# A graph attention kernel: weight sums, pair loads and result additions of the second product put elsewhere

## The chip, the cores and the metric

The kernel runs on one core of one Trainium2 chip. The metric is the device time of one execution in microseconds (us), of which the median over runs is given; lower is better. Everything is computed in 32-bit floats.

## The reference

Two graph attention layers on 512 nodes and 768 features, then a residual addition and a layer norm. The first layer has H = 8 heads of 768 features each, the second has one.

```python
def gat_layer(x, W, a_s, a_d, b, edge_index, concat):
    h = (x @ W).reshape(n, H, C)
    alpha_s = einsum('nhc,hc->nh', h, a_s); alpha_d = einsum('nhc,hc->nh', h, a_d)
    e = leaky_relu(alpha_s[src] + alpha_d[dst], 0.2)
    alpha = softmax of e over the edges of one dst
    out = segment_sum(h[src] * alpha, dst)
    return out + b
h = elu(gat_layer(x, W1, a_src1, a_dst1, b1, edge_index, concat=True))     # 512 x 6144
out = gat_layer(h, W2, a_src2, a_dst2, b2, edge_index, concat=True)        # W2 is 6144 x 768
return layernorm(x + out)
```

## The kernel before

The edges are counted once into a dense 512 x 512 matrix, so that attention is dense. Heads go one after another through a pipeline of three kinds of stages on TensorE:

- a *projection*: HS[h] = x @ W1 of a head (512 x 768 times 768 x 768);
- a *mixed* stage: the head's features times its turned attention weights PT, followed by elu, into gT (`mixed`);
- a *second* stage: h2 += gT of this head times its 768 rows of W2 (`second_by_thirds`), while scores of the next head are computed on VectorE and ScalarE and turned by DMA transposes (`turn_out`, `turn_in`).

In the loop `for h in range(H - 1)` come mixed(h), second(h) and, where there still is a head h + 2, its projection. For h = 1 to 5 that is `project_by_thirds`; for h = 0 it is `projection` (fourteen products by halves). The last head (h = 7) is done after the loop by halves (`second`), then come the second layer's attention and the layer norm.

**Products by thirds.** Left operand, weights and result are cut in parts (two row blocks of 256 nodes, three blocks of 256 inputs, three of 256 outputs), and 15 products P0 to P14 of sums of such parts replace 18. Each product is two row tiles times two input tiles: the page counts 8 matmuls for it. The results of products accumulate in five chains, each with one PSUM bank: a (P8), x (P13, P4, P6, P14, P7), b (P9), y (P2, P12, P0, P10, P11, P3), z (P1, P5). After each product the bank's present content is added to, or subtracted from, one part of the destination; the next product of the same chain may not begin before that has read the bank. `STEPS` (L423) names the chain, the part (row block, column block) and the sign of each product.

**How a result gets to its part of h2** (`empty` in `by_thirds`). Either VectorE adds the bank to h2 (L461), or, for the parts listed in `by_dma`, ScalarE copies the bank into a pass buffer (L458) and GpSimd issues an accumulating DMA from there into h2 (L459). Before, the parts are (1, 2), (0, 1) and (0, 2), so the results of P8, P13, P0, P1, P14, P11 and P3 go by DMA: seven in a stage with h > 0, and four in h = 0, where the first result of each part is copied straight into h2 by ScalarE. There are two pass buffers, the halves of `pass_`. In h = 0 `pass_` first holds the left operands P8 and P13; for h > 0 the tile `absent` holds them.

**The weight operands.** Each of the 15 products needs a weight part or a sum of parts. The slot w1 holds those of the second product, the slot w2 those of the projection. A slot has the rows (`w1r`, 6 tiles of 128 x 768: chunk 0 holds P8, P9, P5; chunk 1 P7, P1, P0; chunk 2 P4, P14, P3), and three flat tiles of two squares each: t1 (P13, P12: "the pairs"), t2 (P6, P2) and t4 (P11, P10). Sums are made by loading one part and adding another from memory with an accumulating DMA on GpSimd's queue (L144), by an accumulating DMA between tiles of the slot, or by VectorE (L170):

- from memory: P1 += , P14 += , P13 += , P12 += , P11 += ;
- then P6 = P14 - P4, P2 = P12 - P13, P4 = P13 + P4, P0 = P12 + P0, P10 = part + P1, P3 = P10 - P3, P1 = P6 + P1, P7 = P6 + P7.

In slot w1, before, P6, P2, P4 and P3 are done by VectorE; P0, P10, P1 and P7 by DMA. `load_thirds` issues all loads of a head in this order: six rows (with the adds into P1 and P14 after the 4th and 6th), then the pairs, each with its add, then `rest`: P11, P10 and the add into P0. For the second product both are called after product n = 14 of the second stage of the head before (and once ahead of the loop, at n = 10 there). The sums P6 and P2 are done in the projection at n = 13 and 14, P4 at the end of the mixed stage (`behind`); P10, P1, P7 are issued in `behind_it[2]`, after product n = 2 of the second stage (L1118); P3 at n = 11.

The products of a second stage run in the order P8, P13, P2, P4, P12, P9, P6, P0, P1, P10, P5, P14, P11, P7, P3 (n = 0 to 14). `plan[n]` is what VectorE and ScalarE are given after product n is issued and ahead of its result, `behind_it[n]` what follows its result. Left operand sums (`gsums`) are part of it; so are, for the next head's four query tiles, `score` (ScalarE: L604), `scored` (VectorE: L608, L613; ScalarE: L617) at n = 5, 7, 9, 11 and `out_by_dma` at n = 7, 9, 11, 13 (ScalarE: L862, L865; SP: a transpose, L867). `turn_in` (ScalarE, L870) takes a transpose in.

**Queues.** The order on every engine is that of the program text; an engine waits in order. Plain loads are issued on SP, accumulating DMAs on POOL. SP also carries the transposes, the row of logits (L596, L599) and, for h = 1 to 5, the reload of five left operands of the projection into gT (`reload_x`, L1003), at n = 11, followed at n = 12 by the load of the w2 slot's P11 (`rest_of_thirds`).

Of the kernel before, what the change touches and what calls it, by code (L numbers as in the profile page):

```python
# [37 lines left out]
def gat_pass(  # L38
# [93 lines left out]
    def load_thirds(m, slot):  # L132

        chunks = CHUNKS[slot]

        def part(k, n):
            lo, hi = chunks[k]
            return m[lo * P:(hi + 1) * P, n * TH:(n + 1) * TH].rearrange("(k p) d -> p k d", p=P)[:, ::hi - lo]

        def flat(j):  # L140
            return wpool.tile([P, HK, HALF], F32, name=f"{slot}t{j}").rearrange("p k n -> p (k n)")

        def add_up(o, i):
            nc.gpsimd.dma_start(o, i, accum_op=ALU.add)  # L144

        rows_, pair_ = wpool.tile([P, DC, D], F32, name=f"{slot}r"), flat(1)
        for j, c in enumerate(c for pair in chunks for c in pair):
            nc.sync.dma_start(rows_[:, j, :], m[c * P:(c + 1) * P, :])
            if j == 3:
                add_up(third(rows_, 1, 1), part(1, 2))  # L150
            if j == 5:
                add_up(third(rows_, 2, 1), part(0, 1))
        for j, (k0, k1, n) in enumerate(((0, 2, 2), (0, 1, 0))):
            nc.sync.dma_start(square(pair_, j), part(k0, n))
            add_up(square(pair_, j), part(k1, n))
        raw = {(k, n): third(rows_, k, n) for k in range(3) for n in range(3)}
        B_ = dict(P8=raw[0, 2], P9=raw[0, 0], P5=raw[0, 1], P13=square(pair_, 0), P12=square(pair_, 1),
                  P14=raw[2, 1], P4=raw[2, 0], P0=raw[1, 2], P3=raw[2, 2], P7=raw[1, 0], P1=raw[1, 1])

        def rest():  # L160

            two, four = flat(2), flat(4)
            B_.update(P6=square(two, 0), P2=square(two, 1), P11=square(four, 0), P10=square(four, 1))
            nc.sync.dma_start(B_["P11"], part(0, 1))
            if slot == "w1":
                nc.sync.dma_start(B_["P10"], part(0, 1))
            add_up(B_["P11"], part(1, 1))

            def op(o, a, b, how):
                return lambda: nc.vector.tensor_tensor(B_[o], B_[a], B_[b], op=how)  # L170

            def by_dma(o, i):
                return lambda: add_up(B_[o], B_[i])
            ops = dict(P6=op("P6", "P14", "P4", ALU.subtract), P4=op("P4", "P13", "P4", ALU.add),
                       P2=op("P2", "P12", "P13", ALU.subtract), P3=op("P3", "P10", "P3", ALU.subtract))
            if slot == "w1":
                add_up(B_["P0"], B_["P12"])
                ops.update(P10=by_dma("P10", "P1"), P1=by_dma("P1", "P6"), P7=by_dma("P7", "P6"))
            else:
                ops.update(P10=op("P10", "P5", "P1", ALU.add), P0=op("P0", "P12", "P0", ALU.add),  # L180
                           P1=op("P1", "P6", "P1", ALU.add), P7=op("P7", "P6", "P7", ALU.add))
            return ops
        return B_, rest
# [4 lines left out]
    def load_w2(h, slot="w1"):  # L188
        return load_w(W2, h, slot, w2[h * D:(h + 1) * D, :])
# [10 lines left out]
    first_rows = wpool.tile([P, DC, D], F32, name="w1r")  # L200
    W1[0] = [first_rows[:, :HK], first_rows[:, HK:]]
# [17 lines left out]
    W1[0].append(wpool.tile([P, HK, HALF], F32, name="w1t1"))  # L219
# [3 lines left out]
    def sums_by_dma(W_, m, slot):  # L223

        lo_, hi_, t1_ = W_
        t2, t4 = (wpool.tile([P, HK, HALF], F32, name=f"{slot}t{j}") for j in (2, 4))
# [1156 lines left out]
```

## Time and profile before

| | us |
|---|---|
| median of 3 runs | 723.98 (723.26 to 726.53) |
| the profiled execution, its own time | 719.46 |
| its span, to which the profile's times and shares refer | 717.6 |
| busy: TensorE / its weight loads | 644.5 / 492.7 |
| busy: VectorE / ScalarE / GpSimd | 515.7 / 337.4 / 178.0 |
| DMA: moved, mean rate | 133.46 MB, 186 GB/s |

The profile's page lists groups of instructions: line, engine, operation, output <- inputs, tile shapes, count, then busy time in us, mean ns of one, and the idle time of the engine just before them with what ended it. PE is TensorE, PEld its weight loads, DVE VectorE, ACT ScalarE, POOL GpSimd, SP the engine that issues plain DMAs; a q behind the engine means its sequencer or queue. Digits are dropped from tile names, so w1t stands for w1t1, w1t2 and w1t4, h for h2. In a timeline the bracket tells how long the engine sat idle before an instruction, and what released it.

### The profile page before, as it was taken

The numbers are of one execution on the slowest core, as the hardware profiler recorded it, in microseconds if no ns is written. First come the engines' busy times: TensorE is split into PE (matmuls) and PEld (weight loads), VectorE is DVE, ScalarE is ACT, GpSimd is POOL, SyncE is SP. The second block draws the span as 40 slices with busy tenths as digits, with TensorE's granted clock in tenths as the row PEclk, the third lists the DMA queues.
The fourth block names the chain that finished last, engine by engine and source line by source line (L and its number), as shares of the span: only waits on it lengthen the run. The fifth ranks groups of instructions, "written<-read, shape, count | busy, mean of one in ns | idle before, by whom it ended". The sixth has DMA issues, their size and how long they took to land.

```text
span 717.6 us, 8533 instructions
## 1 busy us (share of the span) xinstructions
PE 644.5 (90%) x2761; PEld 492.7 (69%) x2761; DVE 515.7 (72%) x1102; ACT 337.4 (47%) x594; POOL 178.0 (25%) x200
## 2 busy tenths in 40 slices
PE   8999993899979996799959998798979999699996
PEld 4555773657868885688848887586767878554653
DVE  8899896387966888367846879366694678538675
ACT  6765863431646164442637154451446326344350
POOL 1300222140342332323331432323332231320000
PEclk9999998799999999899989999899899999899998
DMA  8982899499878996699967997599957994662021
GB/s 306 303 188 75 242 246 223 78 264 264 221 101 188 267 239 166 107 271 274 236 104 156 275 249 191 89 224 258 231 138 132 284 297 94 103 161 43 12 69 70
DMA packets 115713, 133.46 MB, mean 186 GB/s; under 512 B 42006, under 2 KB 96846, under 8 KB 114894
## 3 DMA queue, kind: packets, MB, share of 16 engines
q1 hardware_dynamic: 75406, 90.63, 40.7%
q0 software_dynamic: 39824, 41.62, 37.8%
q10 hardware_dynamic: 432, 0.59, 0.3%
q8 instruction: 24, 0.39, 0.2%
q14 instruction: 27, 0.22, 0.1%
HBM read 99.25 MB, written 2.90 MB: 142 GB/s over the span
## 4 chain that ended last, share of the span: by engine, by line
PE 55%; DMA 19%; DVE 15%; issue 5%; ACT 4%; SPq 1%; POOL 1%; DVEq 0%; POOLq 0%; ACTq 0%
PE mm L448 22%; PE mm L942 13%; PE mm L380 13%; DMA w1t<-in_L_gnn_W_dram 5%; DMA w1r<-w1t 4%; DMA w1r<-in_L_gnn_W_dram 4%; DVE h L461 3%; PE mm L1329 3%; DMA h<-pass 3%; DVE q L608 2%; PE held L380 2%; DVE q L613 2%; DMA gT<-xd 1%; DMA w2t<-in_L_gnn_W_dram 1%; PE tr L710 1%
## 5 line engine op out<-in xcount | busy, mean ns | idle before, releaser
L459 POOL DMA_DIRECT2D h<-pass x46 | 62.3, 1354 | 185.0 <-ACT pass L458 126.3
L448 PE MATMUL mm<-w1r,gS 128*128 128x256 f32 x168 | 52.7, 469 | 53.4 <-DMA w1r<-w1t 53.0
L461 DVE TENSOR_TENSOR h<-h,mm 128x512 f32<-128x512 f32 x53 | 36.3, 685 | 82.7 <-PE mm L448 80.9
L448 PEld LDWEIGHTS mm<-w1r,gS 128*128 128x128 f32 x168 | 37.8, 233 | 65.2 <-DMA w1r<-w1t 55.8
L942 PE MATMUL mm<-PT,hs 128*128 128x256 f32 x252 | 62.2, 383 | 0.0
L617 ACT ACTIVATE q<-q,nmax 128x512 f32<-128x512 f32 x32 | 23.0, 720 | 72.7 <-DVE nmax L613 72.7
L454 ACT ACTIVATE hs<-mm 128x512 f32<-128x512 f32 x30 | 17.9, 597 | 77.7 <-PE mm L448 64.4
L942 PEld LDWEIGHTS mm<-PT,hs 128*128 128x128 f32 x252 | 48.4, 192 | 7.4 <-ACT u L946 0.3
L461 DVE TENSOR_TENSOR hs<-hs,mm 128x512 f32<-128x512 f32 x45 | 30.8, 685 | 31.3 <-PE mm L448 31.3
L870 ACT COPY PT<-zr 128x1024 uint16<-128x1024 uint16 x34 | 39.2, 1156 | 17.4 <-DMA zr<-nr 16.7
L942 PE MATMUL mm<-pS,gS 128*128 128x256 f32 x168 | 43.3, 380 | 0.0
L458 ACT ACTIVATE pass<-mm 128x512 f32<-128x512 f32 x46 | 26.3, 584 | 35.1 <-PE mm L448 29.0
L448 PE MATMUL mm<-w1t,hs 128*128 128x256 f32 x168 | 42.6, 400 | 0.0
L144 POOL DMA_DIRECT2D w1r<-w1t x21 | 25.2, 1358 | 64.5 <-DMA w1t<-in_L_gnn_W_dram 30.2
L448 PE MATMUL mm<-w1r,hs 128*128 128x256 f32 x168 | 39.3, 383 | 1.2 <-ACT pass L458 1.2
L448 PEld LDWEIGHTS mm<-w1t,hs 128*128 128x128 f32 x168 | 35.1, 209 | 6.0
L144 POOL DMA_DIRECT2D w1r<-in_L_gnn_W_dram x14 | 16.8, 1199 | 84.9 <-DMA w1r<-in_L_gnn_W_dram 34.3
L448 PE MATMUL mm<-w2r,xT 128*128 128x256 f32 x160 | 37.8, 379 | 0.0
L448 PE MATMUL mm<-w2r,gT 128*128 128x256 f32 x160 | 37.5, 382 | 0.0
L448 PEld LDWEIGHTS mm<-w1r,hs 128*128 128x128 f32 x168 | 31.3, 190 | 7.5 <-ACT pass L458 3.6
L942 PEld LDWEIGHTS mm<-pS,gS 128*128 128x128 f32 x168 | 32.2, 192 | 4.5
L946 ACT COPY u<-mm 128x256 f32<-128x256 f32 x21 | 7.8, 371 | 56.7 <-PE mm L942 56.7
(271 smaller groups left out, 1536.4 us busy)
## 6 DMA issues: line engine op xcount, KB each, us to landing
w2r<-in_L_gnn_W_dram SPq DMA_DIRECT2D x48, 384.0 KB
w1r<-in_L_gnn_W_dram SPq DMA_DIRECT2D x43, 384.0 KB
h<-pass POOLq DMA_DIRECT2D x46, 256.0 KB, 5.2
w1t<-in_L_gnn_W_dram SPq DMA_DIRECT2D x28, 256.0 KB
gT<-xd SPq DMA_DIRECT2D x5, 1280.0 KB
w1t<-in_L_gnn_W_dram POOLq DMA_DIRECT2D x21, 256.0 KB, 6.5
w1r<-w1t POOLq DMA_DIRECT2D x21, 256.0 KB, 5.0
w2t<-in_L_gnn_W_dram SPq DMA_DIRECT2D x15, 256.0 KB
```

Source lines behind the costliest of these rows:

```text
L144: nc.gpsimd.dma_start(o, i, accum_op=ALU.add)
L380: nc.tensor.matmul(ps[:, :HALF], A_[p][:, k, i * P:(i + 1) * P], B_[p][:, k, :], start=start and k == 0, stop=k == HK - 1, skip_group_chec ...
L448: nc.tensor.matmul(bank[chain][:, i * TH:(i + 1) * TH], A_[p][:, k, i * P:(i + 1) * P], B_[p][:, k, :], start=first and i == k == 0, stop= ...
L454: nc.scalar.activation(out(o), ps, AF.Copy, scale=sign)
L458: nc.scalar.activation(part, ps, AF.Copy, scale=sign)
L459: nc.gpsimd.dma_start(out(o), part, accum_op=ALU.add)
L461: nc.vector.tensor_tensor(out(o), out(o), ps, op=ALU.add if sign > 0 else ALU.subtract)
L608: nc.vector.scalar_tensor_tensor(q, q, NEG_SLOPE, q, op0=ALU.mult, op1=ALU.min)
L617: nc.scalar.activation(q, q, AF.Exp, bias=nmax, scale=-1.0, accum_out=dens[t])
L870: nc.scalar.copy(PT.rearrange("p s n -> p (s n)").bitcast(U16).rearrange("p (s n h) -> p s n h", s=NT, h=2)[:, :, t * P:(t + 1) * P, :], p ...
L942: nc.tensor.matmul(bank[p][:, :HN], A_[p][:, k, c * P:(c + 1) * P], B_[p][:, k, :], start=over is None and k == 0, stop=k == 1, skip_group ...
L1329: nc.tensor.matmul(ps[:, :cols.stop - cols.start], PT[:, s, t * P:(t + 1) * P], h2[:, s, cols], start=(s == 2), stop=(s == 1))
```

## The change

- In slot w1, P1 = P6 + P1 is done by VectorE instead of a DMA, and P10 += P1 is issued right behind the loads. P0 += P12 and P7 += P6 still go by DMA. P2 moves to n = 12 of the projection and P6 to n = 14; P4 and P1 follow at the end of the next mixed stage (`behind`). For h = 0, where P2 alone is done in the mixed stage, P6, P4 and P1 are done at n = 0, 1 and 3 of the second stage; for h = 1 P4 and P1 are.
- The pairs of the next head's second product are loaded at n = 5 of the second stage; the first two rows at n = 13, behind the reload of gT and the load of the w2 slot's P11, which both move there from n = 11 and 12; the rest at n = 14. The tiles of slot w1 are allocated once, so that a load waits for the readers of its own part alone.
- The parts that go to h2 by DMA are (0, 0), (0, 1) and (0, 2): the results of P2, P7, P1, P14, P11 and P3. Those of P8, P13 and P0 are added by VectorE. In h = 0 three go by DMA.
- There are four pass buffers: the halves of `pass_` and the halves of `absent`, read as 32-bit floats.

```diff
+        def load_rows(k):
+            for j, c in enumerate(chunks[k]):
+                nc.sync.dma_start(rows_[:, 2 * k + j, :], m[c * P:(c + 1) * P, :])
+        def load_pairs():
+            pair_ = flat(1)
+            for j, (p, k0, k1, n) in enumerate((("P13", 0, 2, 2), ("P12", 0, 1, 0))):
+                B_[p] = square(pair_, j)
+                nc.sync.dma_start(B_[p], part(k0, n))
+                add_up(B_[p], part(k1, n))
...
+    def load_second(h):
+        B_, part, load_rows, load_pairs, load_four, ops = thirds_of(w2[h * D:(h + 1) * D, :], "w1", w1_sums.get, w1_rows)
+        def load_rest():
+            load_rows(1)
+            add_up(B_["P1"], part(1, 2))
+            load_rows(2)
+            add_up(B_["P14"], part(0, 1))
+            add_up(B_["P0"], B_["P12"])
+            load_four("P11", "P10")
+            add_up(B_["P10"], B_["P1"])
+        ops["P7"] = lambda: add_up(B_["P7"], B_["P6"])
+        return B_, ops, load_pairs, lambda: load_rows(0), load_rest
...
-    W1[0] = [first_rows[:, :HK], first_rows[:, HK:]]
+    w1_rows = wpool.tile([P, DC, D], F32, name="w1r")
+    w1_halves = {j: wpool.tile([P, HK, HALF], F32, name=f"w1t{j}") for j in (1, 2, 4)}
+    w1_sums = {j: t_.rearrange("p k n -> p (k n)") for j, t_ in w1_halves.items()}
+    W1[0] = [w1_rows[:, :HK], w1_rows[:, HK:]]
...
-                         h == 0, ((1, 2), (0, 1), (0, 2)))
+                         h == 0, ((0, 0), (0, 1), (0, 2)))
...
-    passed = [pass_[:, j] for j in range(2)]
+    veiled = absent.rearrange("p t n -> p (t n)").bitcast(F32).rearrange("p (j n) -> p j n", j=2)
+    passed = [t_[:, j] for t_ in (pass_, veiled) for j in range(2)]
...
-            B2, rest_of_w2 = load_thirds(w2[:D, :], "w1")
-            sums2 = rest_of_w2()
+            B2, sums2, load_pairs, load_first, load_rest = load_second(0)
+            load_pairs()
+            load_first()
+            load_rest()
...
-    behind, in_second, in_third = [sums2.pop("P6"), sums2.pop("P2")], [], {}
+    behind, in_second, in_third = [sums2.pop("P2")], [], {}
...
-        plan = {0: of_b("P4") + sum_up("P14") + finish[:1], 1: finish[1:] + sum_up("P12", "P9"), 2: sum_up("P7"),
-                3: sum_up("P1") + at(score, 0), 4: sum_up("P6"), 5: at(scored, 0) + at(score, 1), 6: sum_up("P3"),
+        plan = {0: of_b("P6") + sum_up("P14") + finish[:1], 1: of_b("P4") + finish[1:] + sum_up("P12"), 2: sum_up("P9", "P7"),
+                3: sum_up("P1") + of_b("P1") + at(score, 0), 4: sum_up("P6"), 5: at(scored, 0) + at(score, 1), 6: sum_up("P3"),
...
-        behind_it = {2: of_b("P10", "P1", "P7")}
+        behind_it = {1: of_b("P7")}
...
-            if 0 < h and n == 11:
-                reload_x()
-            if 0 < h and n == 12:
-                sums = rest_of_thirds()
+            if n == 5:
+                B2, sums2, load_pairs, load_first, load_rest = load_second(h + 1)
+                load_pairs()
+            if n == 13:
+                if 0 < h:
+                    rest_of_thirds()
+                    reload_x()
+                load_first()
             if n == 14:
-                B2, rest_of_w2 = load_thirds(w2[(h + 1) * D:(h + 2) * D, :], "w1")
-                sums2 = rest_of_w2()
+                load_rest()
...
-                if n in (13, 14):
-                    sums2.pop("P6" if n == 13 else "P2")()
+                if n in (12, 14):
+                    sums2.pop("P2" if n == 12 else "P6")()
...
-            behind = [sums2.pop("P4")]
+            behind = [sums2.pop("P4"), sums2.pop("P1")]
```

More of the change, by code (lines that the diff above doesn't have):

```diff
@@ L153, in load_thirds @@
[L153 to L182, printed above, removed]
@@ L183, in load_thirds, with load_four @@
-        return B_, rest
+        def load_rows(k):
[7 more added lines that the diff above has]
+                add_up(B_[p], part(k1, n))
+        def load_four(*names):
+            four = flat(4)
+            for j, p in enumerate(("P11", "P10")):
+                B_[p] = square(four, j)
+                if p in names:
+                    nc.sync.dma_start(B_[p], part(0, 1))
+            add_up(B_["P11"], part(1, 1))
@@ new lines, in thirds_of, with op, do @@
+        raw = {(k, n): third(rows_, k, n) for k in range(3) for n in range(3)}
+        B_ = dict(P8=raw[0, 2], P9=raw[0, 0], P5=raw[0, 1], P14=raw[2, 1], P4=raw[2, 0], P0=raw[1, 2], P3=raw[2, 2],
+                  P7=raw[1, 0], P1=raw[1, 1])
+        def op(o, a, b, how):
+            def do():
+                if o in ("P6", "P2"):
+                    B_[o] = square(flat(2), ("P6", "P2").index(o))
+                nc.vector.tensor_tensor(B_[o], B_[a], B_[b], op=how)
+            return do
+        ops = dict(P2=op("P2", "P12", "P13", ALU.subtract), P6=op("P6", "P14", "P4", ALU.subtract),
+                   P4=op("P4", "P13", "P4", ALU.add), P10=op("P10", "P5", "P1", ALU.add), P0=op("P0", "P12", "P0", ALU.add),
+                   P1=op("P1", "P6", "P1", ALU.add), P3=op("P3", "P10", "P3", ALU.subtract), P7=op("P7", "P6", "P7", ALU.add))
@@ L1073, in gat_pass @@
         if 0 < h and not last:
[L1074 removed]
+            B3, rest_of_thirds, sums = load_thirds(h + 2)
         elif h:
@@ L1226, in gat_pass @@
     xr = load_x()
-    b2_bc = wpool.tile([P, DC, D], F32, name="w1r")[:, 0, :]
+    b2_bc = w1_rows[:, 0, :]
     nc.sync.dma_start(b2_bc, row_bcast(b2))
```

39 lines of the change are left out of this document (22 added, 17 removed).

## The prediction

> **What bounds the kernel now.** I read the page's groups first, then who TensorE waits for, then busy time per stage, then single engines around the waits. Below, S is the time at which the fifteen products of a second stage (head h) begin and E the time at which they end; after E come the fifteen products of the next projection, then the mixed stage (aggregation) of head h+1, then its second stage.
>
> ```profile
> span 717.6 us, 8533 instructions
> L448 PE MATMUL mm<-w1r,gS 128*128 128x256 f32 x168 | 52.7, 469 | 53.4 <-DMA w1r<-w1t 53.0
> ```
>
> TensorE is busy 90% of the span, so about 73 us are idle; 53.0 of them stand before one group: products with weights in w1r and left operands in gS, released by a DMA from w1t into w1r. The table of stages shows what they cost in all. Columns: stretch, its length, busy time (and instructions) of PE, PEld, DVE, ACT, POOL, then granted clock, DMA share, GB/s. The first seven rows are the second stages of h = 0 to 6, the eighth is one projection of the same fifteen products, the last three are mixed stages.
>
> ```profile
> 100.20:143.80 43.60, 29.97 (x122) 24.68 (x122) 24.77 (x54) 20.51 (x36) 9.81 (x8) 0.84 0.81 191
> 189.20:222.90 33.70, 28.55 (x122) 23.82 (x122) 25.69 (x57) 18.77 (x33) 9.58 (x8) 0.95 0.75 139
> 267.50:305.20 37.70, 28.49 (x121) 23.87 (x121) 24.05 (x54) 18.80 (x33) 9.62 (x8) 0.86 0.68 138
> 350.40:387.20 36.80, 28.49 (x122) 23.85 (x122) 24.07 (x54) 18.76 (x33) 9.61 (x8) 0.91 0.70 143
> 432.00:468.60 36.60, 28.91 (x121) 24.12 (x122) 24.01 (x54) 18.73 (x33) 9.62 (x8) 0.91 0.67 139
> 520.50:554.10 33.60, 28.44 (x121) 23.81 (x121) 24.05 (x54) 18.69 (x33) 9.63 (x8) 0.95 0.65 126
> 600.60:637.50 36.90, 30.13 (x129) 24.98 (x128) 23.45 (x51) 16.96 (x31) 10.81 (x9) 0.91 0.45 73
> 387.20:413.30 26.10, 26.10 (x121) 22.69 (x120) 19.29 (x32) 7.58 (x10) 9.67 (x8) 1.00 1.08 266
> 413.30:432.00 18.70, 18.70 (x86) 15.69 (x84) 14.02 (x33) 11.07 (x25) 6.03 (x5) 1.00 1.00 244
> 494.70:520.50 25.80, 21.58 (x86) 17.63 (x85) 14.32 (x33) 11.06 (x25) 7.29 (x7) 0.87 0.97 226
> 580.30:600.60 20.30, 19.04 (x86) 15.56 (x84) 13.83 (x33) 11.06 (x25) 2.47 (x2) 1.00 0.92 250
> ```
>
> Fifteen products with nothing in their way take 26.10 us at clock 1.00, so one takes 1.74. The seven second stages sum to 258.9 us (43.60+33.70+37.70+36.80+36.60+33.60+36.90), where 7 x 26.10 would be 182.7. The excess of 76.2 is the 53.0 of idle time, the slow clock behind it (0.84 to 0.95 in these rows alone), and some lag. The place in one stage (h = 2; columns: start, us, engine, line):
>
> ```profile
> 281.47 1.70 POOL L144 DMA_DIRECT2D w1t<-w1r  x1
> 286.50 2.41 POOL L144 DMA_DIRECT2D w1r<-w1t  x2 [3.33 <-DMA w1t<-w1r]
> 290.53 3.72 PE L448 MATMUL mm<-w1r,gS 128*128 128x256 f32 x8 [8.96 <-DMA w1r<-w1t]
> ```
>
> P10 += P1 is issued at 281.47, 14 us into the stage; only when it has landed can P1 += P6 go at 286.50; TensorE has waited 8.96 us for it, and its eight matmuls then take 3.72 instead of 1.9. Two dependent transfers, issued too late, set the seven stages.
>
> **Removed.** In the changed kernel P10 += P1 is issued with the stage's loads, before the stage begins, and P1 = P6 + P1 is a VectorE instruction: for h = 1 to 6 at the end of the mixed stage or at n = 3, for h = 0 at n = 3. Both inputs are there by then. So the wait goes, and its clock loss with it: -76.2 at most.
>
> **Added in the second stage.** The prices:
>
> ```profile
> L461 DVE TENSOR_TENSOR h<-h,mm 128x512 f32<-128x512 f32 x53 | 36.3, 685 | 82.7 <-PE mm L448 80.9 <-ACT q L862 1.1
> L170 DVE TENSOR_TENSOR w1r<-w1t,w1r 128x512 f32<-128x512 f32 x14 | 9.6, 684 | 0.0
> L459 POOL DMA_DIRECT2D h<-pass x46 | 62.3, 1354 | 185.0 <-ACT pass L458 126.3 <-DMA h<-pass 29.2 <-ACT q L862 9.0
> ```
>
> Per stage with h > 0, P8, P13 and P0 are now added to h2 by VectorE, P2 and P7 by DMA: 8 results on VectorE become 9, 7 by DMA become 6. With the P1 sum VectorE gains 2 x 0.685 = 1.4 us on 24.05, which still is under 26.1, so it is no bound by sum. But order counts. Up to rank of query tile 1 (n = 7) its queue gains P1, P8, P13 and loses P2: +0.6 x 2 = +1.2 (one ends 0.6 after the last). P0 then follows rank 1. ScalarE is tied to that rank; in h = 3, whose stage starts at 350.5:
>
> ```profile
> 365.35 0.72 ACT L617 ACTIVATE q<-q,nmax 128x512 f32<-128x512 f32 x1 [2.59 <-DVE nmax L613]
> 366.07 0.71 ACT L604 ACTIVATE q<-q,al_d 128x512 f32<-128x512 f32 x1
> 366.68 0.57 ACT L458 ACTIVATE pass<-mm 128x512 f32<-128x512 f32 x1
> 367.16 0.71 ACT L862 ACTIVATE q<-q,rden 128x512 f32<-128x512 f32 x1
> 367.90 1.04 ACT L865 COPY pS<-q 128x1024 uint16<-128x1024 uint16 x1
> ```
>
> P1's pass stands behind this copy. The long wait hid that; now it counts. ScalarE is free at 368.9, less 0.5 for P0's pass, which has left it, plus 1.2: 369.6, and P1's pass ends at 370.2 = S+19.7. P5 shares P1's bank, is due at S+17.4 and waits 2.3. I add 0.1 for later small waits: 2.4 per stage, 28.5 us long. Bounds: nothing, if the rank isn't later and ScalarE catches up, and 4.4 if TensorE's y bank is held up as well, where P10 (n = 9) now waits for P0 on VectorE. In h = 0 four subtractions of counts and three sums of weights (0.68 each) run too, 4.8 us; I take 3.0 of them as uncovered: 31.5 (bounds 28 to 35). New sum: 6 x 28.5 + 31.5 = 202.5; term A = 202.5 - 258.9 = **-56.4**.
>
> Four buffers instead of two cost no instruction. The upper two are the tile absent, whose other readers (P8, P13, the count subtractions) are done at n = 1 or n = 8, before it is written; nothing is added for them.
>
> **Moved.** The pair loads (two on SP, two adds on POOL) move from behind the six rows to n = 5. There SP waits for P12's matmul (n = 4), with only the transposes of n = 7 on behind it, and the DMA share of the second stages is 0.65 to 0.81, so I cost them at nothing. If that cover is gone, P2's sum waits for them in the projection (n = 12), at most the 3.7 us that it waits now. In return the reload of gT and the load of P11 move behind the last transpose on SP, and P6 moves to n = 14 of the projection. First the loads on SP (h = 3, whose stage ends at 387.2, and h = 4, which ends at 468.6), and from the chain of waits what the queue does with them:
>
> ```profile
> 386.29 0.52 SPq L1003 DMA_DIRECT2D gT<-xd  x1
> 388.06 1.61 SPq L867 DMA_TRANSPOSE zr<-nr  x1
> 467.90 0.53 SPq L1003 DMA_DIRECT2D gT<-xd  x1
> ...
> 467.90 8.78 DMA gT<-xd
> 476.69 13.89 DMA w1r<-in_L_gnn_W_dram
> ```
>
> Then who needs what lands: VectorE's sums P6 (412.94, 496.81) and P2 (501.84), and TensorE in the projection (400.98) and the mixed stages:
>
> ```profile
> 412.94 0.69 DVE L170 TENSOR_TENSOR w1t<-w1r 128x512 f32<-128x512 f32 x1 [0.15 <-issue]
> 496.81 0.69 DVE L170 TENSOR_TENSOR w1t<-w1r 128x512 f32<-128x512 f32 x1 [2.60 <-issue]
> 501.84 0.69 DVE L170 TENSOR_TENSOR w1t<-w1t 128x512 f32<-128x512 f32 x1 [3.74 <-DMA w1t<-in_L_gnn_W_dram]
> ...
> 400.98 1.89 PE L448 MATMUL mm<-w2r,gT 128*128 128x256 f32 x8
> 498.20 1.03 PE L942 MATMUL mm<-pS,gS 128*128 128x256 f32 x4
> 503.45 2.08 PE L942 MATMUL mm<-pS,hs 128*128 128x256 f32 x4 [4.22 <-DVE w L953]
> 585.94 1.13 PE L942 MATMUL mm<-pS,hs 128*128 128x256 f32 x4 [1.18 <-DVE w L953]
> ```
>
> Reload, rows and the add into P14 follow each other in the queue (8.78, then 13.89, then the add), and P6 = P14 - P4 waits for the last. From reload to P6 it took 26.7 us (386.29 to 412.94) and 28.9 (467.90 to 496.81). Now the reload goes after the transpose: that is issued at E+0.9 (388.06), 0.7 later for P7's pass ahead of it on ScalarE, takes 1.61, and P11's load 0.4; so it goes at E+3.9, and P6 at E+30.6 to E+32.8. After P6 (0.69), P3's result (0.69), u and w (0.41 each, half a 512-wide one) TensorE gets its bank at E+32.8 to E+35. It stops, as at 498.20+1.03, 4.5 us into the mixed stage, at E+30.6. So each of five mixed stages waits 2.2 to 4.4. P2's wait (3.74 at 501.84) goes, as its pair is loaded 30 us earlier. I take 2.4 for four of them, and 4.4 with 3 us of slow clock for the one that is like h = 4: 17.0. Gone are the losses of before, 25.80 and 20.30 against 18.70: 8.7. Term B = **+8.3** (bounds -8.7, if the rows land in time, and +28, if all five are like h = 4).
>
> [...]
>
> The reloaded gT is first read at 400.98, E+13.8. It would land at E+3.9+8.8 = E+12.7, 1.1 early, with the load of P11 ahead of it and more adds beside it. Term C = five times 0.5 = **+2.5** (bounds 0 and 5 x 3 = 15).
>
> The tail after the last second stage waits for adds into h2, now P14, P11, P7, P3, before P14, P11, P3; P7 goes beside P11 on its way. I take nothing, bounds -2 and +4.
>
> **Sum.** The profiled execution took 719.46 us (span 717.6): 719.46 - 56.4 + 8.3 + 2.5 = 673.9. The median shown, 723.98, is 4.5 above it; with the same 4.5 the forecast is **678**.
>
> **Rivals.**
> - *Lag in VectorE and ScalarE fills the second stage.* For it: DVE has 25 us of work in 28. If the upper bounds hold, 6 x 30.5 + 35 = 218: 15.5 worse, **694**. Against it: before the wait, eight products ran without a gap.
> - *Late rows in all five mixed stages.* DMA share is 1.08 in the projection, over 1.00 in the mixed stage beside it. If all are like h = 4: 5 x 7.4 = 37 instead of 17, **698**.
> - *No new wait.* ScalarE keeps up and the reload is early: 19.8 of lag and 2.5 go, **656**.
> - *Slower: the adds queue up on POOL's queue.* Adds are issued in one order there: P14, P11, P7, P3 into h2, the one for P11, then P1 and P14 of the weights, from E-3.5 on. How long one takes, in the second stage and then in the projection of h = 2 (last number, us to landing):
>
> ```profile
> h<-pass POOLq DMA_DIRECT2D x5, 256.0 KB, 3.8
> h<-pass POOLq DMA_DIRECT2D x2, 256.0 KB, 10.4
> ```
>
>  If seven went one by one at 7 us, P14 would land at E-3.5+49 = E+45.5, 14.5 after E+31, five times: 72 us, **751**. It eats the whole gain from 6.2 us each (E+40, five times 9.1). Against it: they overlap, two went on together at 286.50. [...]
> - *The change doesn't do what it says:* P1's sum overwrites what P10 += P1 reads, so it waits for that last add. At E+31 plus three more at 3.8 that lands at E+42; the sum is due near E+49, so it is early by 7. If it were 2 us late in six stages: **690**.
>
> **How the numbers follow.** Forecast 0.55 (own range 662 to 690), lag 0.13, late rows 0.12, no new wait 0.08, not as it says 0.02, slower 0.08; 0.02 is left for no change. Range 656 to 704, which leaves out about 0.15: the slower case, no change, and the ends of the others. What the measurement can tell is about 0.5%, 3.6 us; faster 0.90, same 0.02, slower 0.08.
>
> **What would show it.** Right: no TensorE idle before P1 of the second stages; those 27 to 30 us long at clock near 1.00 (h = 0 at 31); waits of 0.5 to 2.5 us before P5 put down to ScalarE's pass; P6's sum waiting for a DMA into w1r at the end of the projection and TensorE for w (L953) in mixed stages. Wrong: waits for DMA again before products with gS, second stages over 32 us, gaps over 2 us at the ninth product of the projection, or mixed stages over 27 us.

## The result, and the profile after

| | before | after |
|---|---|---|
| median of the runs side by side, us | 725.08 (723.26 to 726.53) | 660.26 (659.72 to 664.08) |
| ratio to before, 95% interval | | 0.9119 [0.9076, 0.9161] |
| profiled execution / its span, us | 719.46 / 717.6 | 659.72 / 657.9 |

Medians here and below are of all executions, while the ratios leave out those over 1.5% above the fastest of their kernel, so that the ratios of before_p1 and late_pairs_p2_last stand for about 670 us (0.9262 x 723.97) and 681 us (0.9388 x 725.12).

The page of after, parts 1 and 2: span, busy time and share of each engine, then TensorE's busy tenths and granted clock in 40 slices:

```profile
span 657.9 us, 8563 instructions
PE 631.3 (96%) x2761; PEld 481.3 (73%) x2761; DVE 523.4 (80%) x1116; ACT 333.1 (51%) x587; POOL 160.8 (24%) x186
...
PE   8999998999989999999999999999999999898995
...
PEclk9999998999999999999999999999999999999998
```

TensorE waits for nothing long any more. The view of waits, TensorE's alone (engine, output and line that waited, releaser; us in total, times, longest):

```profile
PE mm L477 <- DVE hs L1073: 5.3, 6, 1.7
PE mm L477 <- DVE h L490: 3.9, 7, 2.0
PE tr L1288 <- DVE tr L1285: 2.6, 1, 2.6
...
PE mm L477 <- ACT pass L487: 1.2, 6, 0.2
PE mm L477 <- ACT absent L487: 1.0, 5, 0.2
```

The DMA waits before P1 have gone and so have the waits for w in the mixed stages. What is left sits before the products (L477, L448 before): left-operand sums (L1073), results that VectorE adds into h2 (L490), passes by ScalarE (L487). By stage, from the view by windows (busy us of each engine, granted clock, DMA share, GB/s) for the second stage of h = 0, the projection that follows the second stage of h = 2, a mixed stage, the second stage of h = 3, and the end of the tail:

```profile
99.40:131.50 32.10, 29.21 (x122) 23.60 (x122) 29.98 (x63) 19.39 (x34) 7.40 (x6) 0.95 1.04 258
280.70:307.00 26.30, 26.30 (x123) 22.68 (x122) 18.71 (x31) 8.00 (x11) 10.93 (x9) 1.00 1.00 255
307.00:325.40 18.40, 18.40 (x85) 15.61 (x83) 14.15 (x33) 11.08 (x25) 6.05 (x5) 1.00 1.04 257
325.40:354.10 28.70, 27.30 (x121) 22.45 (x121) 25.41 (x56) 17.63 (x31) 5.98 (x5) 1.00 0.79 167
...
596.50:657.90 61.40, 52.04 (x187) 30.75 (x185) 42.22 (x89) 19.30 (x30) 0.00 (x0) 0.97 0.15 44
```

The whole span, cut where TensorE's first matmul of each stage starts, against the prediction's terms:

| us | before | after | difference | predicted |
|---|---|---|---|---|
| up to the first second stage | 100.2 | 99.4 | -0.8 | 0 |
| second stages, h = 0 / 1 / 2 to 5 / 6 | 259.0 | 32.06 + 30.32 + 114.96 + 30.06 = 207.4 | -51.6 | -56.4 (A) |
| mixed stages, h = 1 to 6 | 120.5 | 110.7 | -9.8 | +8.3 (B) |
| projections, h = 0 to 5 | 157.8 | 158.2 | +0.4 | +2.5 (C) |
| last aggregate and tail | 80.1 | 82.2 | +2.1 | 0 |
| span | 717.6 | 657.9 | -59.7 | -45.6 |

The mixed stages are the surprise: none waits. The lag within a second stage has about its predicted length (28.7 us, where the projection's fifteen products take 26.2), but it is made of several short waits, the longest in another place than predicted. The second stage of h = 2, TensorE's timeline:

```profile
257.67 1.99 PE L477 MATMUL mm<-w1r,gT 128*128 128x256 f32 x8 [0.21 <-DVE h L490]
...
269.03 1.99 PE L477 MATMUL mm<-w1t,hs 128*128 128x256 f32 x8 [0.73 <-DVE hs L1073]
271.23 3.72 PE L477 MATMUL mm<-w1r,hs 128*128 128x256 f32 x16 [0.20 <-ACT absent L487]
...
278.92 1.99 PE L477 MATMUL mm<-w1r,hs 128*128 128x256 f32 x8 [0.19 <-ACT pass L487]
280.75 1.89 PE L477 MATMUL mm<-w2r,xT 128*128 128x256 f32 x8
```

These are P4 (n = 3; two expectations below call it P9), P10 (n = 9), P5 with P14 (n = 10, 11), P3 (n = 14) and the projection's first product. P4 waits for P13's result, which VectorE adds to h2, and P10 for its left-operand sum on VectorE; P5, for which 2.3 us were predicted, waits 0.20 for P1's pass.

### The profile page after: what moved, and what is told of

It is laid out like the page before. It is cut to its first block, busy times and chain, and to the rows that moved or that the text cites. A ratio compares the mean times of both kernels' runs of the same rounds, so it can differ in the third digit from the quotient of the medians.

```text
span 657.9 us, 8563 instructions
## 1 busy us (share of the span) xinstructions
PE 631.3 (96%) x2761; PEld 481.3 (73%) x2761; DVE 523.4 (80%) x1116; ACT 333.1 (51%) x587; POOL 160.8 (24%) x186
## 5 line engine op out<-in xcount | busy, mean ns | idle before, releaser
L490 DVE TENSOR_TENSOR hs<-hs,mm 128x512 f32<-128x512 f32 x45 | 30.8, 685 | 43.2 <-PE mm L477 43.2
L646 ACT ACTIVATE q<-q,nmax 128x512 f32<-128x512 f32 x32 | 23.1, 720 | 68.6 <-DVE nmax L642 68.6
L133 POOL DMA_DIRECT2D w1t<-in_L_gnn_W_dram x21 | 32.2, 1582 | 67.8 <-DMA w1t<-in_L_gnn_W_dram 48.4
L490 DVE TENSOR_TENSOR h<-h,mm 128x512 f32<-128x512 f32 x60 | 41.0, 683 | 9.5 <-PE mm L477 9.0
L477 PE MATMUL mm<-w1t,hs 128*128 128x256 f32 x168 | 40.4, 383 | 5.3 <-DVE hs L1073 5.3
L488 POOL DMA_DIRECT2D h<-pass x20 | 26.0, 1370 | 76.6 <-ACT pass L487 56.8
L477 PE MATMUL mm<-w1r,hs 128*128 128x256 f32 x168 | 40.0, 386 | 2.3 <-ACT pass L487 1.2
L488 POOL DMA_DIRECT2D h<-absent x19 | 24.5, 1366 | 68.0 <-ACT absent L487 58.1
L477 PE MATMUL mm<-w1r,gS 128*128 128x256 f32 x168 | 40.4, 383 | 0.4
L477 PEld LDWEIGHTS mm<-w1t,hs 128*128 128x128 f32 x168 | 31.3, 190 | 12.0 <-DVE hs L1073 8.0
L477 PEld LDWEIGHTS mm<-w1r,hs 128*128 128x128 f32 x168 | 30.8, 190 | 10.8 <-ACT pass L487 3.6
L477 PE MATMUL mm<-w2r,gT 128*128 128x256 f32 x160 | 37.9, 385 | 0.0
L477 PE MATMUL mm<-w2r,xT 128*128 128x256 f32 x160 | 37.8, 379 | 0.0
L477 PEld LDWEIGHTS mm<-w1r,gS 128*128 128x128 f32 x168 | 31.3, 190 | 7.2 <-ACT pass L487 1.9
L477 PEld LDWEIGHTS mm<-w2r,gT 128*128 128x128 f32 x160 | 29.6, 190 | 6.6 <-DVE hs L490 3.0
L477 PEld LDWEIGHTS mm<-w2r,xT 128*128 128x128 f32 x160 | 30.4, 190 | 4.1
```

Source lines behind the costliest of these rows:

```text
L477: nc.tensor.matmul(bank[chain][:, i * TH:(i + 1) * TH], A_[p][:, k, i * P:(i + 1) * P], B_[p][:, k, :], start=first and i == k == 0, stop= ...
L488: nc.gpsimd.dma_start(out(o), part, accum_op=ALU.add)
L490: nc.vector.tensor_tensor(out(o), out(o), ps, op=ALU.add if sign > 0 else ALU.subtract)
L646: nc.scalar.activation(q, q, AF.Exp, bias=nmax, scale=-1.0, accum_out=dens[t])
```

## The experiments

Each run is a whole kernel, three rounds (five for the last two) beside the kernel before. Medians, ratios with their 95% intervals, and stage lengths of the profiled execution:

| run | median us | ratio | second stages h = 0 / 1 / 2 to 5 (mean) | projections h = 1 to 5 (mean) | mixed h = 2 to 6 |
|---|---|---|---|---|---|
| changed | 660.26 | 0.9119 [0.9076, 0.9161] | 32.1 / 30.3 / 28.7 | 26.2 | 18.4 18.4 18.5 18.4 18.4 |
| before_p1 | 676.51 | 0.9262 [0.9161, 0.9362] | 32.0 / 31.3 / 28.7 | 26.1 | 18.9 18.5 24.2 24.9 26.3 |
| p1_by_dma | 668.76 | 0.9248 [0.9192, 0.9303] | 40.8 / 29.9 / 28.8 | 26.2 | 18.5 each |
| early_reload | 659.95 | 0.9109 [0.9051, 0.9167] | 32.1 / 30.3 / 28.8 | 26.2 | 18.4 each |
| late_pairs | 709.34 | 0.9798 [0.9738, 0.9858] | 32.1 / 30.3 / 28.8 | 35.7 | 18.4 19.7 18.7 18.4 18.5 |
| late_pairs_p2_last | 683.66 | 0.9388 [0.9298, 0.9478] | 32.1 / 30.3 / 28.7 | 26.1 | 23.0 26.9 24.1 23.4 26.6 |
| two_buffers | 667.65 | 0.9242 [0.9173, 0.9312] | 32.1 / 30.3 / 28.8 | 26.8 | 18.4 each |
| old_parts | 668.53 | 0.9235 [0.9179, 0.9291] | 41.8 / 31.3 / 28.7 | 26.2 | 18.4 each |
| sums_moved | 659.43 | 0.9097 [0.9039, 0.9155] | 30.2 / 30.0 / 28.5 | 26.2 | 18.5 18.4 18.5 18.4 23.1 |
| sums_moved_last | 656.41 | 0.9078 [0.9024, 0.9132] | 30.2 / 30.0 / 28.5 | 26.2 | 18.4 each |
| sums_moved_copy_late | 654.62 | 0.9005 [0.8929, 0.9080] | 30.0 / 29.4 / 27.9 | 26.2 | 18.4 18.4 18.4 18.4 22.4 |
| all_moves | 649.75 | 0.8984 [0.8938, 0.9030] | 29.6 / 29.0 / 27.4 | 26.2 | 18.4 to 18.5 |
| changed_again | 661.32 | 0.9152 [0.9095, 0.9209] | 32.1 / 30.3 / 28.8 | 26.2 | 18.4 each |

Where mixed stages wait, executions of one kernel lie further apart: 665.67 to 681.68 for before_p1, 678.22 to 691.42 for late_pairs_p2_last, and the profiled one is the longest of each. Their mixed stages are read for which wait it is; for its mean size the medians count.

**P1 alone, in the kernel before (before_p1).**

```diff
-                ops.update(P10=by_dma("P10", "P1"), P1=by_dma("P1", "P6"), P7=by_dma("P7", "P6"))
+                add_up(B_["P10"], B_["P1"])
+                ops.update(P1=op("P1", "P6", "P1", ALU.add), P7=by_dma("P7", "P6"))
...
-                3: sum_up("P1") + at(score, 0)
+                3: sum_up("P1") + of_b("P1") + at(score, 0)
-        behind_it = {2: of_b("P10", "P1", "P7")}
+        behind_it = {2: of_b("P7")}
```

> The kernel before, with only the sum P1 of the second product moved to VectorE (at n = 3) and P10 += P1 issued with the load; reload, order of the loads, parts by DMA and the two buffers stay as before. Theory 'chain': the whole gain of the second stages (259 to 207 us in the profiles) comes from no longer waiting for P10 += P1 and P1 += P6 one behind the other, so the second stages come to 205 to 215 us, the mixed stages keep their waits for P2's pair (two of 20 to 26 us), and the time is 672 to 680. Rival 'early pairs and parts matter too': VectorE's P1 now waits for its rows or for P10 += P1, second stages of 225 us or more, time 690 to 705.

676.51, about 670 by its ratio: the chain theory. The second stages have about the lengths of the changed kernel, 208.7 us in all for 207.4. Its waits, TensorE's and those of VectorE's weight sums (L170; P2 waits for w1t, P6 for w1r):

```profile
DVE w1t L170 <- DMA w1t<-in_L_gnn_W_dram: 14.5, 4, 5.3
...
PE mm L449 <- ACT pass L459: 14.1, 17, 2.6
...
PE mm L943 <- DVE w L954: 13.6, 4, 5.2
...
DVE w1t L170 <- DMA w1r<-in_L_gnn_W_dram: 7.1, 4, 3.4
```

Two things are to be seen. With the old parts and two buffers the lag is a wait for ScalarE's passes (14.1 us). And the wait for w stays, and what VectorE waits for ahead of w is mostly P2's pair (14.5 us against 7.1). The faster second stage doesn't make that go; something else in the change did.

**VectorE, or the place in POOL's queue (p1_by_dma).**

```diff
+        ops["P1"] = lambda: add_up(B_["P1"], B_["P6"])
...
-            behind = [sums2.pop("P4"), sums2.pop("P1")]
+            behind = [sums2.pop("P4")]
-        behind_it = {1: of_b("P7")}
+        behind_it = {1: of_b("P1", "P7")}
```

> The changed kernel with P1 += P6 back on an accumulating DMA, issued at n = 1 of the second stage, ahead of P7 += P6, while P10 += P1 stays with the load. Theory 'place in the queue': one add of 4 to 5 us that starts 3 us into the stage is there long before P1's matmul (16 us into it); no wait comes back, VectorE saves 0.7 us in each mixed stage, 657 to 661 us. Rival 'engine': what counted was VectorE; TensorE waits for the DMA before P1 in each second stage, 3 to 8 us in seven stages, 680 to 715 us.

668.76, between the two. From h = 1 on nothing comes back: the place in the queue was enough. In h = 0 one wait comes back (the view of waits, then the timeline):

```profile
PE mm L478 <- DMA w1r<-w1t: 7.6, 1, 7.6
```

```profile
111.20 2.95 POOL L133 DMA_DIRECT2D w1r<-w1t  x2
...
126.12 3.42 PE L478 MATMUL mm<-w1r,gS 128*128 128x256 f32 x8 [7.64 <-DMA w1r<-w1t]
```

There the DMA share is high (1.12 from 111.2 to 126.1 in the changed kernel), and the add issued at 111.2 let P1 go at 126.1, 14.9 us later; the prediction's rows had 3.8 and 10.4.

**The reload back at n = 11 (early_reload).**

```diff
+            if 0 < h and n == 11:
+                reload_x()
+            if 0 < h and n == 12:
+                rest_of_thirds()
             if n == 13:
-                if 0 < h:
-                    rest_of_thirds()
-                    reload_x()
                 load_first()
```

> The changed kernel with the reload of gT at n = 11 and the load of P11 at n = 12 of the second stage again, ahead of the last transpose, as before the change. Theory 'counted twice': the rows come no earlier, since the last transpose then stands between reload and rows; the add into P14 still lands 20 to 22 us after the end of the second stage, P6's sum doesn't move and the time is 659 to 662. Rival 'less traffic': the rows came in time only because other transfers left that window; then the reload's earlier place brings the add into P14 to 15 to 18 us after the stage's end, and the time is the same or 1 to 2 us less. Rival 'the reload was better before': gaps in the projection go, under 657.

659.95, the same time. SP's queue at the end of the second stage of h = 2, first this run (next stage from 281.58), then the changed kernel (from 280.75), with POOL's add into P14 behind (start, us, engine, line):

```profile
280.83 0.52 SPq L1033 DMA_DIRECT2D gT<-xd  x1
281.44 0.42 SPq L159 DMA_DIRECT2D w2t<-in_L_gnn_W_dram  x1
282.96 2.57 SPq L897 DMA_TRANSPOSE zr<-nr  x1
285.62 3.81 SPq L145 DMA_DIRECT2D w1r<-in_L_gnn_W_dram  x6
...
299.05 1.21 POOL L133 DMA_DIRECT2D w1r<-in_L_gnn_W_dram  x1 [1.72 <-PE mm L477]
```

```profile
282.12 1.23 SPq L897 DMA_TRANSPOSE zr<-nr  x1
283.45 1.26 SPq L159 DMA_DIRECT2D w2t<-in_L_gnn_W_dram  x1
284.80 0.46 SPq L1033 DMA_DIRECT2D gT<-xd  x1
285.35 3.61 SPq L145 DMA_DIRECT2D w1r<-in_L_gnn_W_dram  x6
...
301.84 1.21 POOL L133 DMA_DIRECT2D w1r<-in_L_gnn_W_dram  x1 [2.42 <-PE mm L477]
...
307.49 0.68 DVE L170 TENSOR_TENSOR w1t<-w1r 128x512 f32<-128x512 f32 x1
```

The transpose is in the queue ahead of the rows in both. Medians over h = 1 to 5, in us after the first matmul of the projection:

| | reload | first row issued | add into P14 issued | P6's sum | P2's sum |
|---|---|---|---|---|---|
| before | -0.9 | 3.6 | 20.3 | 25.8 | 28.9 |
| early_reload | -0.9 | 3.2 | 19.9 | 26.7 | 23.1 |
| changed | 4.1 | 4.6 | 21.6 | 26.7 | 23.1 |
| late_pairs_p2_last | 3.9 | 4.5 | 21.6 | 27.2 | 32.7 |

Reload 5.0 later, rows 1.4 and the add 1.7 later: counted twice, as far as rows and add go. The add came a little earlier than before only in part of the heads, so less traffic explains little. P6 has no bracket at 307.49 (its place in VectorE's order is all that it waits for), and in the run with the early reload it starts no sooner. In the changed kernel P6 also stands one product later, at n = 14; no run moves P6 alone, so how much that hides is not known.

**Late pairs, with P2 where the change puts it (late_pairs) and where it was (late_pairs_p2_last).**

```diff
             add_up(B_["P14"], part(0, 1))
+            load_pairs()
             add_up(B_["P0"], B_["P12"])
...
                 B2, sums2, load_pairs, load_first, load_rest = load_second(h + 1)
-                load_pairs()
```

```diff
-                if n in (12, 14):
-                    sums2.pop("P2" if n == 12 else "P6")()
+                if n in (13, 14):
+                    sums2.pop("P6" if n == 13 else "P2")()
```

> The changed kernel with the pairs P13 and P12 loaded behind the add into P14 again, so after the rows and not amid the second stage. Theory: the pairs were not what gained in the second stage, but P2's sum (n = 12 of the projection) then waits for its pair, and P0 += P12 and P11's add stand behind them in POOL's queue: 0 to 4 us of wait in each of five mixed stages, 662 to 678 us. Rival 'pairs are free anywhere': the waits of before came from the late rows alone, 659 to 661 us. Where the pairs amid the stage slowed its own adds, the second stages become shorter than 207 us together.

> The run with the late pairs, with VectorE's sums at the end of the projection in the order of before too: P6 at n = 13, P2 at n = 14. Theory 'only the place of the waiting sum': of the 49 us that late pairs cost, most came because VectorE stood at n = 12 of the projection, ahead of the results that free its banks; with P2 last the projections come back to 26.2 us and the five mixed stages lose what they lost in the run with P1 alone (0.5 to 8 us each, 20 together) plus what the reload behind the last transpose adds, 0 to 3 us each: 678 to 695 us. Rival 'late pairs cost the same anywhere': 700 to 712 us. Rival 'P2's place alone': no loss, under 664 us.

709.34, far worse than any theory had it, and 683.66. In the first P2's sum holds up VectorE amid the projection, and with it the results that free TensorE's banks; here that wait of TensorE, and P2's longest in VectorE's timeline:

```profile
PE mm L478 <- DVE hs L491: 38.0, 5, 9.8
```

```profile
571.94 0.69 DVE L170 TENSOR_TENSOR w1t<-w1t 128x512 f32<-128x512 f32 x1 [9.88 <-DMA w1t<-in_L_gnn_W_dram]
```

In the second the projections are whole and the mixed stages pay, again for P2 (320.26) more than for P6 (313.61):

```profile
PE mm L973 <- DVE w L984: 19.8, 5, 5.5
```

```profile
313.61 0.69 DVE L170 TENSOR_TENSOR w1t<-w1r 128x512 f32<-128x512 f32 x1 [2.29 <-issue]
...
320.26 0.69 DVE L170 TENSOR_TENSOR w1t<-w1t 128x512 f32<-128x512 f32 x1 [5.36 <-DMA w1t<-in_L_gnn_W_dram]
```

So the early pairs are worth 683.66 - 660.26 = 23 us by the medians with P2 last (about 20 by the ratios, 0.9388 against 0.9119), and 49 with P2 at n = 12: without them, P2 at n = 12 holds up every projection from h = 1 on.

**Two buffers, and the old parts (two_buffers, old_parts).**

```diff
-    passed = [t_[:, j] for t_ in (pass_, veiled) for j in range(2)]
+    passed = [pass_[:, j] for j in range(2)]
...
-                         h == 0, ((0, 0), (0, 1), (0, 2)))
+                         h == 0, ((1, 2), (0, 1), (0, 2)))
```

The first run has the first edit, the second both.

> The changed kernel with two buffers for the passes into h2 instead of four, parts as changed. Theory 'buffers matter at the end': P14, P11, P7 and P3 go by DMA within 6 us, and with two buffers P7's pass waits until the add of P14 has landed (3.8 to 5 us after its issue) and P3's until that of P11; ScalarE is held up with the copy of the last query tile behind it, 1 to 4 us in each of seven second stages, 667 to 690 us. Rival 'spare room': the adds land in time, 659 to 663 us.

> The changed kernel with two buffers and the old parts by DMA (P8, P13, P0 / P1, P14, P11 / P3): seven adds in a stage instead of six, P2, P12 side by side on VectorE as before. Against the run with two buffers and the new parts it shows the parts alone. Theory: three adds at the end of a stage (P14, P11, P3) instead of four need no more than two buffers, and VectorE has one result less at its busiest place: 655 to 664 us. Rival 'the parts were needed': P13's pass waits for P8's add or P0 finds P13's add unfinished, ScalarE and then P9 and P10 are late, 670 to 690 us.

667.65 and 668.53. Four buffers bring 7 us; between the old and the new parts there is no difference that can be told. The loss lies mainly in h = 0: with the new parts 5.1 us in its projection (32.2 after 27.1), where P7's pass waits for its buffer, with the old parts 9.7 in its second stage. There, from the run with the old parts, ScalarE's passes of P0 and P11 and POOL's queue:

```profile
117.75 0.57 ACT L487 ACTIVATE pass<-mm 128x512 f32<-128x512 f32 x1
...
126.58 1.20 POOL L133 DMA_DIRECT2D w1t<-in_L_gnn_W_dram  x1 [12.47 <-PE mm L477]
128.91 1.19 POOL L133 DMA_DIRECT2D w1t<-in_L_gnn_W_dram  x1 [1.13 <-DMA w1t<-in_L_gnn_W_dram]
129.62 2.94 POOL L488 DMA_DIRECT2D h<-pass  x2
...
137.19 0.60 ACT L487 ACTIVATE pass<-mm 128x512 f32<-128x512 f32 x1 [8.77 <-DMA h<-pass]
```

The pair adds, now issued amid the stage, stand in POOL's queue for 12.5 us. P0's add, whose pass was done at 118.3, goes behind them at 129.6, 11 us after its pass; the passes stand behind their buffers (8.77 us in the second), and the bank of TensorE behind the passes (5.77 us before P3, at 137.84). With four buffers and the new parts, the changed kernel, this stage takes 32.1 us instead of 41.8.

**Where the lag sits, and a faster version (sums_moved, sums_moved_last, sums_moved_copy_late, all_moves).** The edits, one on top of the other:

```diff
-        plan = {0: of_b("P6") + sum_up("P14") + finish[:1],
-                6: sum_up("P3"), 8: sum_up("P10", "P5"), 10: sum_up("P11"),
+        plan = {0: of_b("P6") + finish[:1],
+                6: sum_up("P10"), 8: sum_up("P5", "P14"), 10: sum_up("P11", "P3"),
```

```diff
-                elif o in by_dma:
+                elif o in by_dma and p not in kept:
...
+                kept = ("P14", "P11", "P7", "P3") if h + 2 == H else ()
```

```diff
-                1: of_b("P4") + finish[1:] + sum_up("P12"), 2: sum_up("P9", "P7"),
+                1: of_b("P4") + finish[1:], 2: sum_up("P12", "P9", "P7"),
-            if n in (7, 9, 11, 13): out_by_dma((n - 7) // 2)
+            if n in (8, 9, 11, 13): out_by_dma((n - 7) // 2)
```

and in all_moves tile 2 at n = 12 too, with the edit of early_reload.

> The changed kernel with left-operand sums in another order: P10's at n = 6 where P3's was, P14's at n = 8 instead of n = 0, P3's at n = 10. Nothing is added or removed. Theory 'the lag sits in P10's sum on VectorE' (0.7 us in each second stage, 1.7 in one, put down to it by the waits before L477): these 5.3 us go, and some of the 3.9 us that P9 (n = 3) waits for P13's result; 651 to 656 us. Rival 'ScalarE takes over': as predicted, P1's pass stands behind the copy of query tile 0, so P5 (n = 10) waits instead and nothing is gained, 659 to 662 us.

> The same, and in the last second stage P14, P11, P7 and P3 are put into h2 by VectorE, not by DMA. Theory 'the tail waits for the adds' (the logits of h2 wait 5.9 us for the last add, TensorE then 2.6 us for its transposes): the tail's 2.0 us come back, 1.5 to 2.5 us under the run with the sums moved alone. Rival: the logits are hidden behind TensorE's aggregate anyway, no difference over 0.5 us.

> The run with the sums moved and the last stage on VectorE, with two things more: ScalarE scales and copies query tile 0 at n = 8, behind P1's pass, instead of n = 7 ahead of it; and P12's left-operand sum goes to n = 2, behind P13's result. Theory 'P5 waits for P1's pass behind that copy': the 1.05 to 1.2 us before P5 (n = 10) fall to 0.2 in six stages, and the waits of P9 (n = 3) for P13's result fall by 0.2 to 0.6; second stages of 27.5 us, 649 to 653 us. Rival: the copy of tile 0, or the tiles behind it, now stand before P14's or P11's pass and P11, P7 or P3 wait as long; 655 to 658 us.

> The run before (sums moved, last stage on VectorE, query tile 0 copied behind P1's pass) with two more moves: query tile 2 is scaled and copied at n = 12, behind P11's pass, and the reload of gT and the load of P11 go back to n = 11 and 12, ahead of the last transpose. Theory 'P7 waits for P11's pass behind the copy of tile 2': its 0.9 to 1.5 us (n = 13) fall to 0.2 in six stages; and the add into P14 goes out about 2 us earlier after the stage's end, so P6's sum at the end of the projection doesn't wait in the last of them (4.3 us there, and 4 us longer in the mixed stage). Second stages of 27.0 us, mixed stages all 18.4, 645 to 650 us. Rival: the later transpose of tile 2 and the reload get in each other's way and the rows are late again, 652 to 657 us.

> The changed kernel itself, on the same chip, for the comparison: 658 to 662 us, 0.909 to 0.914 of the kernel before. If it is not within that, the differences of 1 to 2 us between the runs here can't be told from the chip's.

sums_moved: 659.43, nothing to be told from the changed kernel; within the stages of h = 2 to 5 the rival (28.5 us for 28.7). In the stage of h = 2 P10's wait is gone and P5 waits instead, behind P1's pass, which ScalarE does after the copy of query tile 0 (L895):

```profile
266.39 1.99 PE L477 MATMUL mm<-w1t,hs 128*128 128x256 f32 x8
...
267.84 1.05 ACT L895 COPY pS<-q 128x1024 uint16<-128x1024 uint16 x1
268.79 0.59 ACT L487 ACTIVATE absent<-mm 128x512 f32<-128x512 f32 x1
...
269.44 3.72 PE L477 MATMUL mm<-w1r,hs 128*128 128x256 f32 x16 [1.05 <-ACT absent L487]
```

With the copy behind the pass (sums_moved_copy_late, 654.62) P5 waits for nothing, and the stage falls from 28.5 to 27.8; now P7 waits for P14's pass:

```profile
266.77 3.62 PE L477 MATMUL mm<-w1r,hs 128*128 128x256 f32 x16
...
273.04 1.99 PE L477 MATMUL mm<-w1r,gS 128*128 128x256 f32 x8 [0.93 <-ACT absent L487]
```

So the prediction's wait was real and stood second, 1.05 us long where 2.3 was forecast. (This run moves P12's sum too, so the fall is not the copy's alone.) all_moves, 649.75, is 0.8984 [0.8938, 0.9030] of before, against 0.9152 [0.9095, 0.9209] for the changed kernel beside it: the fastest. Its expectation named the wrong pass: P7's 0.94 stayed, since P14's pass stands behind the exponentials of tile 3 and not behind a copy; what went is P3's 0.19. sums_moved_last gave 3.0 us by medians; the tail's wait for L1285 (2.6 in the changed kernel) isn't among its waits. That its interval overlaps that of sums_moved leaves the size open.

The table shows one thing more: the last mixed stage took 23.1 us in sums_moved and 22.4 in sums_moved_copy_late, for 18.4 elsewhere. There P6's sum waited for the add into P14, from VectorE's timeline in sums_moved and, with the same instructions up to that place, in sums_moved_last:

```profile
530.09 0.69 DVE L170 TENSOR_TENSOR w1t<-w1r 128x512 f32<-128x512 f32 x1 [4.86 <-issue]
```

```profile
525.45 0.68 DVE L170 TENSOR_TENSOR w1t<-w1r 128x512 f32<-128x512 f32 x1
```

The add was issued at 521.0 in the first and at 519.9 in the second, and landed 9.0 us after its issue in the one and 4.6 in the other. So the add is in time with little to spare (in changed_again P6 waits 0.25 and 0.81 in two heads, at no cost), and one execution can lose what another does not: the profiled one of sums_moved has second stages 3.0 us shorter in all than the changed kernel's, and this wait cost it 4.7. In all_moves every mixed stage took 18.4. There the same add landed 7.4 us after its issue and was still in time, since it was issued 18.8 us into the projection (21.6 is the median of the changed kernel). This speaks for the early reload, but sums_moved_last has 18.4 everywhere without it.

## Why the prediction came out as it did

678 was forecast, 660.26 measured: inside the whole range of 656 to 704, but 17.7 below the forecast and under the 662 to 690 that it gave as its own. Of this, 14.2 is the sum (673.9 against the profiled 659.72); the rest is the offset between profile and median, 0.5 here where 4.5 was taken. Within the sum term B was 18.1 too high and A 4.8 too low, so the sum is nearer than its parts by luck; what C and the tail missed by cancels.

**Term A, right in its mechanism.** The wait for P10 += P1 and P1 += P6 one behind the other was the bound: P1 alone makes the second stages nearly those of the changed kernel. -51.6 against -56.4: h = 1 took 30.3 and h = 6 30.1, both taken as 28.5, and h = 0 32.1 for 31.5. The lag of 2.4 is nearly right for h = 2 to 5 (28.7 against 28.5), in part by luck: one wait of 2.3 before P5 was forecast, and 0.73 before P10, 0.20 before P5 and smaller ones came. Its place was half right: "P1's pass stands behind this copy" holds, but VectorE was later still, at P10's sum, which the prediction didn't follow. Two waits in a row didn't add: taking away P10's 0.73 (sums_moved) showed 1.05 before P5, and the stage fell by 0.2.

**Term B, the step that failed.** "so it goes at E+3.9, and P6 at E+30.6 to E+32.8" carried the time from reload to P6, 26.7 and 28.9, along with the reload. The reload does go at E+4.1 (the times given for it, 0.9, 0.7, 1.61 and 0.4, add up to 3.6, not 3.9). But those 26.7 us held the last transpose, which now stands ahead of the reload: it was counted twice. And in the first of the two stages P6 had not waited for rows (its bracket there is 0.15), so the interval was VectorE's and not the queue's. P6 came at E+26.7, with no wait, so that the 17.0 us put on the mixed stages did not come: 18.1 us of error in this term. The 17.0 counted four of these waits, of 2.4 each, at full clock, which no run shows: in late_pairs_p2_last a wait of 2.35 (ended at 240.75) left the next four matmuls at 1.13 us, but the two fours behind them took 2.07 and 1.75, where four take 1.03 in the changed kernel. Beside that, the price set on losing the early pairs' cover was too low, at most 3.7 us: the run late_pairs_p2_last shows that without them the mixed stages lose 4.6 to 8.5 us each in its profiled execution (23.0 to 26.9 for 18.4), and 20 to 23 in all. That is no part of the 18.1, since the forecast had P2's wait gone.

**Term C** was on the side of its lower bound: no wait at the ninth product, +0.4 for 2.5. **The tail** was taken at 0 with bounds -2 and +4: +2.1. The logits of h2 wait for the last add there (VectorE's timeline, then the chain of waits, both of after):

```profile
587.90 0.96 DVE L424 SCALAR_TENSOR_TENSOR scr<-h,w2t 128x768 bf16<-128x768 f32 x1 [5.91 <-DMA h<-absent]
```

```profile
576.48 11.33 DMA h<-absent
```

It lands 11.3 us after its issue; why so late was not tried. With the last stage's four results on VectorE (sums_moved_last) last aggregate and tail took 79.9 us, for 81.5 in sums_moved and 80.1 before, so the adds are the cause of most of the 2.1; the second stage of h = 6 is 0.7 us longer there than in sums_moved.

**The rivals.** "No new wait", 656, came nearest, and by luck: its sum takes out the lag (19.8) and term C (2.5) and keeps the 17.0 of waits in the mixed stages. It was the lag that stayed (207.4 - 182.7 = 24.7) and those waits that did not come. "Lag fills the second stage" did not come, nor did "late rows" in the changed kernel's profile; in sums_moved and sums_moved_copy_late they did, in one stage of six. "The adds queue up on POOL" is there in h = 0 alone, and shows only with two buffers. "P1's sum waits for that last add": no wait.

**The clock** came back as forecast: 1.00 in the second stage shown by the windows, 0.95 in h = 0. Of the signs named for being right, no idle time before P1 and the lengths of the second stages came; P5's wait of 0.5 to 2.5 us (0.20 here) and the waits for P6's rows and for w did not.

## What to carry to other kernels

Before an interval between two events is moved with one of them, look whether the later one waited at all, and what else stands inside the interval: what is moved out of it must not be counted again. When one sum of a load set is always last, the load that feeds it is worth moving even where it seems hidden (20 to 23 us here), and an add put early on a queue that waits in order needs buffers for all that stands behind it (in old_parts the pair adds stood 12.5 us in POOL's queue, and P0's add behind them). After a wait has been taken away, the next one can already be there: here 0.73 us before P10, then 1.05 before P5, then 0.93 before P7.

## What the runs showed of the hardware

How little idle time lowers TensorE's clock. TensorE's timeline in the changed kernel (h = 0, then h = 1) and in sums_moved (h = 0):

```profile
107.59 3.57 PE L477 MATMUL mm<-w1r,gT 128*128 128x256 f32 x8 [2.01 <-DVE h L490]
...
195.62 1.99 PE L477 MATMUL mm<-w1t,hs 128*128 128x256 f32 x8 [1.71 <-DVE hs L1073]
```

```profile
107.65 1.99 PE L477 MATMUL mm<-w1r,gT 128*128 128x256 f32 x8 [1.41 <-DVE h L490]
```

2.01 us idle and the next eight matmuls take 3.57 instead of 1.99, at a granted clock of 0.55 (window 107.5 to 111.2); 1.41 and 1.71 us left them at 1.99. The same wait of 2.01 us made them 2.72 to 3.65 in five kernels (the changed one, changed_again, p1_by_dma, early_reload, late_pairs_p2_last), and where they took 3.18 or less, the eight behind them took 2.44 to 2.90. Two products ahead of it stand another 0.45 us of idle time; in old_parts 2.45 us, with no other wait over 0.2 in the 7 us before it, made them 3.60. Near 1.9 us it went both ways: 1.90 us in before_p1 were followed by 2.00 and 1.87 in all_moves by 1.99, but 1.87 in sums_moved_copy_late, before the same product as in all_moves, by 3.26. Nearly half of what the second stage of h = 0 takes over those of h = 2 to 5 comes from here: 3.57 - 1.99 = 1.6 of 32.06 - 28.74 = 3.3.
